# A four-layer network: two more turns in a fixed order, and nine shifted copies of the inverse norms

## The chip, the cores and the metric

The kernel runs on one core of a Trainium2 chip, as one launch over a batch of two images of 512 channels and 64 x 64 pixels. The metric is the device time of that launch in microseconds (us), the median of several runs.

## The reference

Four layers, each with a residual and a group normalisation ahead of it. The change lies in the first, an attention over a 3 x 3 neighbourhood and 256 pooled tokens. Cut to that part:

```python
x = x + L0(_gn(x))        # then L1, L2, L3 in the same way
# L0: B=2, C=512, N=64*64 pixels, 8 heads of 64, ws=3, ll=9
q = heads(xf @ W_q + b_q);  q_norm = q / norm(q)
q_scaled = (q_norm + query_embedding) * softplus(temperature)
k_l, v_l = split(xf @ W_kv + b_kv);  k_l = k_l / norm(k_l)     # per head and pixel
k_local, v_local = 3x3 patches of k_l, v_l (zero padded)
attn_local = einsum('bhnd,bhndk->bhnk', q_scaled, k_local)     # nine taps
attn_pool = einsum('bhnd,bhpd->bhnp', q_scaled, l2norm(k_pool))  # 256 pooled tokens
attn = softmax(concat([attn_local, attn_pool]))
lt = q_norm @ learned_tokens + learned_bias + attn[..., :ll]
out = (einsum(lt, v_local) + einsum(attn[..., ll:], v_pool)) @ W_proj + b_proj
```

All values are f32.

## The kernel before

**Units and turns.** `Local.run` (from L2047) does the first layer. The 512 channels are four chunks of 128 (two heads each), the 4096 pixels four strips of 1024 (`UT`), so an image has 16 units of one chunk and one strip, numbered by `u = 4 * chunk + strip`. A turn `i` runs from -4 to 16 and works on several units at once: it projects k and q for unit i+3 (`projections`), brings the inverse norms of what the turn before projected (`norms`, `normed`), forms the nine products of q with shifted k for unit i+1 (`tap_products`, DVE, L2489), sums each product over a head's channels on TensorE (`tap_sums`, L2527), projects v for unit i+1 (`value`), attends with unit i (`attend`: exponentials L2555 and L2559, values L2565, softmax sums L2581 and L2584, reciprocal L2609 to L2617) and weighs the neighbouring values of unit i-1 (`weigh`). Each of these is a generator; `in_turn` advances them in rotation, one step each.

**Orders.** Which instruction stands where on an engine is set by a scheduler, except in turns for which `self.steady` is true: there PE's instructions keep the order in which the generators emit them (`manual_schedule` for PE). `self.steady` also selects another plan of steps: products in pairs of taps (one DVE instruction of 128 x 2048 elements in place of two of 128 x 1024), `halved(1)` into the buffers `sq[2:]` in place of `prob`, other numbers of empty steps, and in `projections` the steps at which k, q and v are projected (`made`, `taken`). Before the change turns 1 to 11 are steady. Turn 13 projects no k and q, and v for the last two units. Turns 14 to 16 attend with the last units and multiply the outputs with the projection (`output`, L2258); `fetch_output` in turn 13 loads that projection into the four `sq` buffers.

**Buffers.** `mm` is a ring of five PSUM banks that nearly everything shares, `tap` is one bank for the tap sums, `qs` two for the q of the products. A tap sum ends with a DVE multiplication by the inverse norms (L2536) and an exponential on ACT (L2538), after which its bank is free. In `weigh`, each of the ten rows of weights of a unit is fetched by two broadcasting DMAs (L2640) into one of three buffers, copied to PSUM by ACT (L2656), multiplied on DVE (L2664) and added by POOL (L2669).

**Inverse norms.** The norm of k belongs to a pixel and a head, and each tap needs it at the neighbour's place. `inverse` is a tensor in device memory. `norms` makes the inverse square roots of a half strip (512 pixels) and stores them by one DMA into six rows: two heads by three shifts in x (L2434). `tap_inverses` reads, for each of four strips of partitions and each of three shifts in y, six rows (L2513): twelve DMAs a unit. Both ends of each row are set to zero at the beginning (L2134). All DMAs here are issued in order by SP.

Of the kernel before, what the change touches and what calls it, by code (L numbers as in the profile page):

```python
# [9 lines left out]
F32 = mybir.dt.float32  # L10
# [8 lines left out]
KC = C // P  # L19
W = 64  # L20
N = W * W
TB = 512
# [20 lines left out]
def bcast(ap, axis, n):  # L43

    a = ap.unsqueeze(axis)
    shape = list(a.shape)
    shape[axis] = n
    return a.to_broadcast(shape)


def in_turn(*gens):


    gens = list(gens)
    while gens:
        gens = [g for g in gens if next(g, gens) is not gens]
# [1911 lines left out]
class Local:  # L1968
# [9 lines left out]
    def __init__(self, net, X, Y, sp_scale, d, wp, yp, pp, ppt, pps):  # L1978
        self.net, self.nc, self.vec, self.cst = net, net.nc, net.vec, net.cst
        self.X, self.Y, self.sp_scale, self.d = X, Y, sp_scale, d  # L1980
        self.wp, self.pp, self.ppt, self.pps = wp, pp, ppt, pps
        nc, new = self.nc, lambda shape, name: wp.tile(shape, F32, name=name)

        self.yd = yp.tile([P, KC, N], F32, name="yd")
        self.edge = W + 1
        self.inverse = yp.tile([6 * KC, N + 2 * self.edge], F32, name="inverse")
        self.wd = yp.tile([3, P, KC, C], F32, name="wd")
        self.rows = cycle([yp.tile([P // 2, self.UT], F32, name=f"rows{i}") for i in range(2)]).__next__

        R = W + 2  # L1990
        flat = Y.rearrange("p k n -> p (k n)")
        self.next_w = flat[:, :KC * C].rearrange("p (kc o) -> p kc o", kc=KC)
        whole = Lent(flat)
        self.kx, self.vx = (whole.take([P, R, R]) for _ in range(2))
        qs, self.kraw = whole.take([P, 3 * self.UT]), whole.take([P, self.UT])
        self.qs = [qs[:, i * self.UT:(i + 1) * self.UT] for i in range(3)]
        weighed = whole.take([P, 2 * self.UT])

        self.taps = ([weighed[:, i * self.UT:(i + 1) * self.UT] for i in range(2)]
                     + [new([P, self.UT], "tap2")])  # L2000
        self.prods = [new([P, 2, self.UT], f"prods{i}") for i in range(2)]
        self.tok = whole.take([P, KC, 32])
        late = new([P, 13 * TB + 3 * TB], "late")
        part = Lent(late)
        self.prob = part.ring([P, TB], 4)
        self.att = part.ring([P, self.UT], 2)
        self.els = part.ring([P, TB], 2)

        self.halves = [part.take([P, TB]) for _ in range(2)]
        self.recip = part.take([P, TB])  # L2010
        self.lts = part.ring([P, TB], 3)

        self.first = Lent(late[:, :12 * TB])
        self.gelus = Lent(late[:, 13 * TB:]).ring([P, TB], 3)
        self.raw_w = [w.rearrange("p (kc o) -> p kc o", kc=KC)
                      for w in (weighed, flat[:, 6144:8192])]
        self.w_sr = qs[:, :KC * C].rearrange("p (kc o) -> p kc o", kc=KC)
        self.fold = flat[:, :6144].rearrange("p (i kc o) -> p i kc o", i=3, kc=KC)
        self.kp = new([P, KC, NK], "kp")
        self.vp = new([P, 2, C], "vp")  # L2020
        self.qn = whole.take([P, self.UT])
        self.w3 = new([P, 3, KC, P], "w3")
        self.sq = [new([P, TB], f"sq{i}") for i in range(4)]
        self.half = new([P, 32], "mhalf32")
        self.qb = new([P, KC], "qe_scaled")
        self.bias = {i: new([P, KC], "b_" + i) for i in "qkv"}
        self.w, self.lt, self.el, self.out = {}, {}, {}, {}
        load = lambda w, src: nc.sync.dma_start(w, src.rearrange("(kc p) o -> p kc o", p=P))
        load(self.w_sr, d["W_sr"])
        for i, src in enumerate((d["W_q"], d["W_kv"][:, :C], d["W_kv"][:, C:])):  # L2030
            load(self.fold[:, i], src)
        for i in range(2):
            load(self.raw_w[i], d["W_kv"][:, i * C:(i + 1) * C])
        nc.sync.dma_start(self.tok, d["tok32"])
        nc.vector.memset(self.half, -0.5)

        nc.vector.tensor_tensor(self.qb, self.vec[:, V_QE:V_QE + KC], sp_scale, ALU.mult)
# [9 lines left out]
    def run(self):  # L2047


        self.nmean = self.net.stats[:, 0]  # L2050
        xs = self.pooled_tokens()
        heads = self.pooled_heads(xs)
        units = KC * self.UN
        unit = lambda u: u if 0 <= u < units else None
        self.pending = []
        for i in "qkv":
            self.fetch(i, 0)
        for i in range(-4, units + 1):
            made, ahead, u, before = (unit(i + n) for n in (3, 1, 0, -1))
            self.steady = 1 <= i < units - 4  # L2060
            streams, ended = [], []
            stages = [self.norms(streams, ended)]
            if ahead is not None:
                stages.append(self.tap_products(ahead))
            if u is not None:
                stages.append(self.attend(u))
            if i == units:
                stages.append(self.output(KC - 2))
            if before is not None:
                stages.append(self.weigh(before))  # L2070
            if ahead is not None:
                stages.append(self.tap_sums(ahead))
            values = ([ahead] if i > 0 and ahead is not None else
                      {-4: [0], -2: [1]}.get(i, []))
            stages.append(self.projections(made, values, streams))
            stages.append(self.normed(ended))
            if i < -2:
                stages.append(islice(heads, 12 if i == -4 else None))
            if i == units - 3:
                stages.append(self.fetch_output())  # L2080
            if units - 3 < i < units:
                stages.append(self.output(i - units + 2))
            if self.steady or i == units:
                with self.net.tc.manual_schedule(engines={mybir.EngineType.PE}):
                    in_turn(*stages)
            else:
                in_turn(*stages)

        self.nc.sync.dma_start(self.next_w, self.d["w_q1"].rearrange("(kc p) o -> p kc o", p=P))
        in_turn(self.output(KC - 1))  # L2090
# [3 lines left out]
    def pooled_tokens(self):  # L2094

        net, nc, w = self.net, self.nc, self.w_sr
# [11 lines left out]
        for blk in range(NB):  # L2108
# [14 lines left out]
            if 1 <= blk <= 3:  # L2123
                i = blk - 1
                w3 = self.fold[:, i]
                net.scale_part(w3, slice(0, KC))
                at = (V_BQ, V_BK, V_BK + KC)[i]
# [2 lines left out]
                nc.sync.dma_start(self.wd[i], w3)  # L2130
        self.frame(self.kx)
        nc.gpsimd.memset(self.kraw[:, :TB], 0.0)
        for at in (0, self.edge - 1 + N):
            nc.sync.dma_start(self.inverse[:, at:at + self.edge + 1],  # L2134
                              self.cst[:6 * KC, :self.edge + 1])
        return xs

    def pooled_heads(self, xs):
# [220 lines left out]
    def projections(self, u, uvs, streams):  # L2359

        nc = self.nc
# [23 lines left out]

            uvs = [last - 1, last]
        values = [(u, j) for u in uvs for j in range(2)]
        made, taken = ((4, 6, 7, 8), (0, 2)) if self.steady else ((6, 7, 8, 9), (0, 3, 6, 9))
        for step in range(10):
            if step in made:  # L2390
                i = made.index(step)
                project("kq"[i // 2], i % 2)
            if step in taken and values:
                v, j = values.pop(0)
# [5 lines left out]
    def norms(self, streams, ended):  # L2400


        nc, wp = self.nc, self.wp
# [10 lines left out]
        n, a = (ps.rearrange("p (b r) -> p b r", r=32)[:, :, 2 * i:2 * i + 2] for i in range(2))  # L2414
# [11 lines left out]
        for s, (which, u, j, part, _) in enumerate(before):  # L2426
            row = rows[32 * s:32 * s + 2, :]
            if which == "q":
                ended.append((s, row, u, j, part))
                continue  # L2430
            at = self.edge + 1 + u % self.UN * self.UT + j * TB
            a = self.inverse[u // self.UN * 6:][:2, at:at + TB]
            heads, cols = a.ap
            nc.sync.dma_start(bass.AP(a.tensor, a.offset, [heads, [2 * heads[0] - 1, 3], cols]),  # L2434
                              bcast(row, 1, 3))
        yield

    def normed(self, ended):
# [67 lines left out]
    def tap_inverses(self, u):  # L2506

        inverse = (self.kraw[:, :TB] if u < KC * self.UN - 1
                   else self.w3[:, 2].rearrange("p k o -> p (k o)"))
        for q in range(4):  # L2510
            for dy in range(3):
                at = u % self.UN * self.UT + q // 2 * TB + dy * W + 1
                self.nc.sync.dma_start(inverse[32 * q + 6 * dy:][:6, :],  # L2513
                                       self.inverse[u // self.UN * 6:][:6, at:at + TB])
        return inverse

    def tap_sums(self, u):
# [348 lines left out]
```

## Time and profile before

| | |
|---|---|
| median of 3 runs | 5019.44 us (5018.50 to 5019.69) |
| profiled execution, its own time | 5015.88 us |
| its span | 5014.0 us, granted TensorE clock 0.984 |
| PE (matmul) busy | 4771.4 us, 95% of the span |
| VectorE (DVE) busy | 3074.1 us, 61% |
| ScalarE (ACT) busy | 1816.8 us, 36% |
| GpSimd (POOL) busy | 1859.1 us, 37% |
| inverse stores and reads | 64 and 384 DMAs of 12 KB |

Busy times are sums over one profiled execution. A row of the table by stretches, used below, gives the start and end of a stretch, its length, then for each engine the busy time and in brackets the number of records, the granted clock of TensorE (PEclk, 1.00 is full speed), the mean busy share of the 16 DMA engines, and GB/s. A 512-column f32 matmul leaves two records, and matmuls on different column strips overlap. A row of waits gives engine and instruction, what ended the wait, the sum in us, how often and the longest. A row of the timeline gives start, length, engine, line, operation, tiles, and in square brackets the idle time ahead of it and what ended it.

### The profile page before, as it was taken

How to read it: one execution, taken by the hardware profiler on the slowest of the kernel's cores; microseconds unless marked ns; L12 is line 12 of the kernel's file. 1: busy time of each engine (PE TensorE's matmuls, PEld its weight loads, DVE VectorE, ACT ScalarE, POOL GpSimd, SP SyncE). 2: the span in 40 equal slices, each digit the busy share in tenths (PEclk: the TensorE clock that was granted, in tenths of full speed). 3: DMA queues.
4: the chain of work that ended last, by engine and by line, in shares of the span. 5: the costliest groups of instructions: out<-in, count | busy, mean ns of one | idle time of the engine just before them, and what ended most of it. 6: DMA issues, size and time to landing. Idle time of an engine off the chain costs nothing. (4 is left out here: it accounts for less than half of the span.)

```text
span 5014.0 us, 48290 instructions
## 1 busy us (share of the span) xinstructions
PE 4771.4 (95%) x16883; PEld 1971.8 (39%) x16883; DVE 3074.1 (61%) x3958; ACT 1816.8 (36%) x3477; POOL 1859.1 (37%) x1220
## 2 busy tenths in 40 slices
PE   7999998999999999999999999989999999999998
PEld 3433332554334444433343333335543344444333
DVE  4367776744679533477732777767446794335776
ACT  1256664244323233322112566642443242333221
POOL 0046665501320145554500466654014101554554
PEclk9999999999999999999999999999999999999999
DMA  3035555500000000211120455555000000000111
GB/s 154 1 103 155 155 156 164 160 19 10 1 17 0 1 1 1 72 55 44 58 74 2 126 154 157 151 159 150 12 10 1 17 1 1 1 1 24 43 45 43
DMA packets 129440, 313.29 MB, mean 62 GB/s; under 512 B 23394, under 2 KB 36194, under 8 KB 127652
## 3 DMA queue, kind: packets, MB, share of 16 engines
q1 hardware_dynamic: 129188, 310.12, 21.6%
q8 instruction: 135, 2.21, 0.2%
q14 instruction: 117, 0.96, 0.1%
HBM read 260.73 MB, written 49.31 MB: 62 GB/s over the span
## 5 line engine op out<-in xcount | busy, mean ns | idle before, releaser
L134 PE MATMUL mm<-big,w 128*128 128x512 f32 x2496 | 1164.9, 610 | 16.3 <-DVE big L2448 11.5
L134 PEld LDWEIGHTS mm<-big,w 128*128 128x128 f32 x2496 | 452.6, 191 | 698.3 <-issue 557.2
L2669 POOL TENSOR_TENSOR late<-late,big 128x1024 f32<-128x1024 f32 x194 | 458.5, 2363 | 223.4 <-DVE big L2664 185.4
L2489 DVE TENSOR_TENSOR prods<-qs,big 128x1024 f32<-128x1024 f32 (+1 forms) x200 | 332.2, 1686 | 60.1 <-PE tap L2527 49.1
L1669 POOL TENSOR_TENSOR big<-big 128x512 f32<-128x512 f32 x224 | 277.8, 1273 | 219.4 <-ACT big L1660 219.4
L2664 DVE TENSOR_TENSOR big<-big,mm 128x512 f32<-128x512 f32 x388 | 253.1, 681 | 114.9 <-ACT mm L2656 107.0
L1660 ACT ACTIVATE big<-mm,ed 128x256 f32<-128x256 f32 x512 | 193.5, 489 | 233.1 <-DVE top L1656 200.7
L2656 ACT COPY mm<-big 128x512 f32<-128x512 f32 x432 | 245.8, 597 | 60.4 <-DMA big<-rows 25.1
L2574 POOL TENSOR_TENSOR late<-late 128x512 f32<-128x512 f32 x84 | 105.3, 1275 | 410.5 <-ACT late L2559 393.9
L2669 POOL TENSOR_TENSOR late<-late,tap 128x1024 f32<-128x1024 f32 x94 | 222.1, 2363 | 94.5 <-DVE tap L2664 80.1
L1472 POOL TENSOR_TENSOR wq<-prob 128x512 f32<-128x512 f32 x48 | 71.6, 1515 | 487.9 <-ACT prob L1469 476.5
L1656 DVE TENSOR_REDUCE top<-mm 128x1 f32<-128x512 f32 x256 | 159.0, 684 | 148.1 <-PE mm L1587 148.1
L1924 PE MATMUL mm<-k,w 128*128 128x512 f32 x512 | 235.1, 602 | 12.4 <-DVE k L1917 7.5
L134 PE MATMUL mm<-big,wq 128*128 128x512 f32 x512 | 236.7, 608 | 2.7 <-ACT off_t L1243 2.7
L1215 PE MATMUL mm<-big,wo 128*128 128x512 f32 x512 | 238.1, 611 | 0.0
L1382 PE MATMUL acc<-big,diag 128*128 128x512 f32 x512 | 228.7, 604 | 9.8 <-ACT diag L1387 4.6
L1634 PE MATMUL mm<-w,big 128*128 128x512 f32 x512 | 234.5, 601 | 0.0
L973 POOL TENSOR_TENSOR group_stats<-group_stats,cst 128x1 f32<-128x1 f32 (+1 forms) x20 | 20.2, 1025 | 566.4 <-DVE group_stats L972 510.2
L2527 PE MATMUL tap<-prods,cst 128*32 128x512 f32 x1152 | 189.6, 620 | 29.2 <-ACT late L2538 26.5
L1914 DVE RECIPROCAL psD<-psD 128x512 f32<-128x512 f32 x64 | 215.1, 3362 | 1.9
L134 PE MATMUL mm<-big,big 128*128 128x512 f32 x464 | 201.7, 594 | 0.5 <-DVE b_sr L1011 0.5
L1469 ACT ACTIVATE prob<-mm 128x512 f32<-128x512 f32 x256 | 133.2, 603 | 171.4 <-PE mm L1466 171.1
(428 smaller groups left out, 8114.1 us busy)
## 6 DMA issues: line engine op xcount, KB each, us to landing
big<-rows SPq DMA_DIRECT2D x432, 256.0 KB
tap<-rows SPq DMA_DIRECT2D x208, 256.0 KB
yd<-late SPq DMA_DIRECT2D x32, 512.0 KB
lost_all<-lost SPq DMA_DIRECT2D x128, 128.0 KB
out<-big SPq DMA_DIRECT2D x64, 256.0 KB
big<-in_W_kv SPq DMA_DIRECT2D x8, 1024.0 KB
rows<-late SPq DMA_DIRECT2D x64, 128.0 KB
big<-in_x SPq DMA_DIRECT2D x32, 256.0 KB
```

The costliest lines, as they stand in the source:

```text
L134: self.nc.tensor.matmul(ps, w[:, kc, :], X[:, kc, blk * TB:(blk + 1) * TB], start=(kc == 0), stop=(kc == KC - 1))
L1215: nc.tensor.matmul(ps, w[:, kc, oc * P:(oc + 1) * P], att[:, kc, :], start=(kc == 0), stop=(kc == KC - 1))
L1382: nc.tensor.matmul(accs[b], dg, src[:, b * TB:(b + 1) * TB], start=(j == 0), stop=(j == 6))
L1634: nc.tensor.matmul(ps, X[:, kc, lo:lo + P], wv[:, kc, :], start=(kc == 0), stop=(kc == KC - 1))
L1660: nc.scalar.activation(f[:, t, :], pS[h][i][:, t % 2, :], AF.Exp, bias=ed[:, t, 2 * cc + h:2 * cc + h + 1])
L1669: nc.gpsimd.tensor_tensor(a, a, part, ALU.add)
L1914: nc.vector.reciprocal(psD, psD)
L1924: nc.tensor.matmul(ps, self.wo[:, kc, oc * P:(oc + 1) * P], qs[:, kc, :], start=(kc == 0), stop=(kc == KC - 1))
L2489: self.nc.vector.tensor_tensor(self.pair(u, k)[:, :n].rearrange("p k (y x) -> p k y x", x=W), bcast(qs.rearrange("p (y x) -> p y x", x=W), ...
L2656: nc.scalar.copy(ps, part)
L2664: nc.vector.tensor_tensor(part.rearrange("p (y x) -> p y x", x=W), self.vx[:, y:y + self.UY // 2, dx:dx + W], ps.rearrange("p (y x) -> p y ...
L2669: nc.gpsimd.tensor_tensor(out, out, t, ALU.add)
```

## The change

`self.steady` holds two turns longer, for turns 1 to 13. In a steady turn up to four value projections find a place (steps 0, 2, 4, 6 instead of 0, 2), which turn 13 uses. `inverse` grows from 6 to 18 rows a chunk: a half strip is stored by three DMAs, one for each shift in y, so that all nine shifted copies stand in memory, and a read takes all 18 rows at once, four DMAs a unit in place of twelve. The zeroed ends grow to fit.

```diff
         self.edge = W + 1
-        self.inverse = yp.tile([6 * KC, N + 2 * self.edge], F32, name="inverse")
+        self.inverse = yp.tile([18 * KC, N + 2 * self.edge], F32, name="inverse")
...
             made, ahead, u, before = (unit(i + n) for n in (3, 1, 0, -1))
-            self.steady = 1 <= i < units - 4
+            self.steady = 1 <= i < units - 2
...
-        for at in (0, self.edge - 1 + N):
-            nc.sync.dma_start(self.inverse[:, at:at + self.edge + 1],
-                              self.cst[:6 * KC, :self.edge + 1])
+        for at in (0, N):
+            nc.sync.dma_start(self.inverse[:, at:at + 2 * self.edge],
+                              self.cst[:18 * KC, :2 * self.edge])
...
-        made, taken = ((4, 6, 7, 8), (0, 2)) if self.steady else ((6, 7, 8, 9), (0, 3, 6, 9))
+        made, taken = ((4, 6, 7, 8), (0, 2, 4, 6)) if self.steady else ((6, 7, 8, 9), (0, 3, 6, 9))
...
-            at = self.edge + 1 + u % self.UN * self.UT + j * TB
-            a = self.inverse[u // self.UN * 6:][:2, at:at + TB]
+            at = 2 * self.edge + u % self.UN * self.UT + j * TB
+            a = self.inverse[u // self.UN * 18:][:2, at:at + TB]
             heads, cols = a.ap
-            nc.sync.dma_start(bass.AP(a.tensor, a.offset, [heads, [2 * heads[0] - 1, 3], cols]),
-                              bcast(row, 1, 3))
+            row_at = heads[0]
+            for dy in range(3):
+                nc.sync.dma_start(bass.AP(a.tensor, a.offset + dy * (6 * row_at - W),
+                                          [heads, [2 * row_at - 1, 3], cols]), bcast(row, 1, 3))
...
         for q in range(4):
-            for dy in range(3):
-                at = u % self.UN * self.UT + q // 2 * TB + dy * W + 1
-                self.nc.sync.dma_start(inverse[32 * q + 6 * dy:][:6, :],
-                                       self.inverse[u // self.UN * 6:][:6, at:at + TB])
+            at = self.edge + u % self.UN * self.UT + q // 2 * TB
+            self.nc.sync.dma_start(inverse[32 * q:][:18, :],
+                                   self.inverse[u // self.UN * 18:][:18, at:at + TB])
```

Lines behind L2434 move by one to three in the changed kernel: L2513 becomes L2514, L2527 L2528, L2555 L2556 and so on; lines ahead of it stay.

## The prediction

> **What bounds the kernel now.** I read the page's busy times first (PE 95% of the span), so a gain has to come out of TensorE's time or its gaps. Then I cut the end of layer 0 at the last softmax-sum matmul (L2584) of each turn, which closes turns 10 to 14 of the first image at 701.75, 743.24, 789.14, 839.46 and 891.85 us, and asked for the busy time of every engine in these stretches:
>
> ```profile
> core 0: us, PE busy (x) PEld busy (x) DVE busy (x) ACT busy (x) POOL busy (x), PEclk, DMA share, GB/s
> 701.75:743.24 41.49, 40.79 (x151) 12.87 (x149) 32.50 (x48) 25.45 (x45) 26.26 (x14) 1.00 0.57 150
> 743.24:789.14 45.90, 45.09 (x162) 14.02 (x160) 34.82 (x55) 26.67 (x47) 28.57 (x15) 1.00 0.52 145
> 789.14:839.46 50.32, 46.00 (x151) 14.58 (x149) 32.25 (x53) 24.98 (x44) 26.05 (x14) 0.93 0.57 157
> 839.46:891.85 52.39, 42.83 (x138) 18.48 (x136) 34.59 (x47) 18.13 (x33) 31.64 (x17) 0.90 0.67 186
> ```
>
> The first row is a steady turn: 41.49 us long, PE busy for 40.79 of them, DVE for 32.5. The next two, turns 12 and 13 in the order that the scheduler chose, hold about the same matmuls (162 and 151 records against 151) and last 45.90 and 50.32 us. In the second image the same stretches last 41.47, 45.03 and 49.94 us.
>
> The same stretches for the nine-tap sums (L2527) alone show one part of the excess:
>
> ```profile
> 701.75:743.24 41.49, 5.31 (x36) 0.77 (x36) 1.00 0.57 150
> 743.24:789.14 45.90, 8.27 (x48) 1.29 (x48) 1.00 0.52 145
> 789.14:839.46 50.32, 8.06 (x36) 1.18 (x36) 0.93 0.57 157
> ```
>
> 36 records cost 5.31 us when they come in fours on four column strips, 8.06 us when the scheduler lets one or two in at a time. TensorE's waits from 743 to 892 us and the timeline ahead of the longest show the other part:
>
> ```profile
> PE tap L2527 <- ACT late L2538: 12.8, 3, 8.2
> PE mm L2258 <- ACT late L2559: 0.7, 1, 0.7
> ...
> 844.36 2.37 DVE L2616 TENSOR_TENSOR late<-late 128x512 f32<-128x512 f32 x1
> 846.77 0.69 DVE L2617 TENSOR_TENSOR late<-late 128x512 f32<-128x512 f32 x1
> 847.38 0.69 DVE L2536 TENSOR_TENSOR tap<-tap,big 128x512 f32<-128x512 f32 x1
> 848.10 0.60 ACT L2538 ACTIVATE late<-tap 128x512 f32<-128x512 f32 x1 [6.83 <-DVE tap L2536]
> 848.75 3.65 PE L2527 MATMUL tap<-prods,cst 128*32 128x512 f32 x16 [8.23 <-ACT late L2538]
> ```
>
> There is one tap bank. The next unit's tap sums wait for the exponential (L2538) of the last unit's, this for L2536, and L2536 stands on DVE behind the whole softmax-reciprocal chain (L2609 to L2617). In turn 13 PE so loses 4.23 us (at 798.07), after it 8.23 us.
>
> **What the Trainium skill says.** "TensorE: Matmul & The Clock Gate", section "What's actually happening": an idle window of about 3.4 us halves the PE clock. The trace agrees: PEclk is 1.00 in steady turns, 0.93 and 0.90 in the rows with the 4.23 and 8.23 us gaps. The same page, "Part 3: Packing small matmuls", section "The mechanism": matmuls on different column strips overlap. The trace agrees: 36 tap records in 5.31 us is 0.15 us each, while a record by itself lasts at least 0.59. "DMA: Bandwidth & Descriptors", section "Two DMAs through the same engine are not ordered": a dependent DMA is issued only when the first one's semaphore has come. The trace agrees: SP holds the second strip's store back until the first has landed (below).
>
> **The change, part by part.** *Turns 12 and 13 steady.* The built program's PE order in them is that of turn 11, matmul for matmul up to turn 13's sums: the four value projections at steps 0, 2, 4, 6 fill slots that steady turns already fill. So each should last a steady turn. First image: 45.90 + 50.32 - 2 x 41.49 = 13.2 us. Second: 45.03 + 49.94 - 2 x 41.47 = 12.0 us. Sum **25.2 us**. DVE's nine products become four pairs and a single at 2.28 us a pair against 2 x 1.22: nothing, and DVE has 9 us of slack in a steady turn.
>
> *The hand-over to turn 14*, which the scheduler still orders. At the end of turn 13's sums the old order has 12 tap records behind it that the new one has not (about 2 us of PE), and unit 15's first four products come before, not after, the reciprocal chain. But PE is starved there anyway, so DVE sets the pace. New DVE chain from the sums' end: 6.2 us to the first L2664 (as in the steady turn, 701.75 to 707.91), six more pairs' halves of L2664 0.6 each, nine single products 1.15 each, L2536 0.6, two L2661 1.2: 6.2 + 3.6 + 10.4 + 0.6 + 1.2 = 22.0 us. Old: 839.46 to the end of L2661 at 862.36 is 22.9 us. Nothing gained or lost, within 1 us; PE stays ill-fed for some 15 us, so a half clock remains there as now. PE idle of about 3.6 us is left before unit 15's first tap sum, then short waits for products.
>
> *SP in turn 13 to 14.* The projection weights for two of the four sq buffers now wait for the sums (which read sq as halves); first use (L2258) is some 25 us later: nothing. The store of unit 12's rows (L2675) moves ahead of the first tap fetches of unit 13. It waits for POOL's last sum, 15.4 us after the sums' end in a steady turn; with 0.4 issue, 4.7 landing and 1.2 copies the fetch is ready at 21.7, against L2661 at 20.8: up to 1 us an image.
>
> *Inverse norms.* 64 stores become 192 and 384 reads become 128, 128 SP issues fewer at about 0.29 us: 37 us of SP time, but SP's waits in a steady turn are for POOL (16.1 us of 41.5), so worth nothing. Three times the stored bytes is 0.8 to 2.4 MB of 313. The two edge fills are larger but come at 38 to 50 us, first read at 251: hidden. The stores also stand closer together:
>
> ```profile
> 729.12 0.43 SPq L2434 DMA_DIRECT2D inverse<-sq  x1
> 730.41 1.08 SPq L2640 DMA_DIRECT2D big<-rows  x2
> 732.10 0.24 SPq L2434 DMA_DIRECT2D inverse<-sq  x1
> 735.14 1.08 SPq L2640 DMA_DIRECT2D big<-rows  x2
> ```
>
> The second strip's store goes 2.98 us after the first, when that one has landed. Now a tap fetch goes in between; in the new order all six stores stand together, so that this fetch (730.41) leaves at about 733.3, some 2.9 us late, in every steady turn. It lands 4.6 us later, at 737.9, where its copy (L2656) runs at 736.98 today; the new ACT order puts these copies after the qs copies (L2483), which follow the last product and so end near 741.7. The PSUM bank that they take (a ring of five, counted through the turn) is freed by L2664 at 740.00 today, some 2.9 us later then, and the matmul that takes it next (L134 at 743.24) has 3.24 us of slack. I take 0 per turn, with -0.1 (fewer issues) and +0.3 as ends, over 22 old steady turns: -2 to +7 us.
>
> *Sum.* The profiled execution took 5015.88 us (span 5014.0): 5015.88 - 25.2 = 4990.7 us. The median of the runs, 5019.44, is 3.6 us above it, so **4994 us**.
>
> **The rivals.**
> 1. *Forecast: the gain of turns 12 and 13 stands at the end.* For it: turns 14 to 16 are PE work behind that front (44.4 of 48.4 us busy in turn 15), and the reciprocal chain, taps and stores all start from the same sums. 4988 to 4999 us. Chance 0.70.
> 2. *Part is given back after turn 13.* Late tap fetches, the half clock running into the first output matmuls (up to 5 us an image at half speed costs 2.5 us), or output loads that the earlier start uncovers. At 3 to 7 us an image: 5000 to 5009 us. Against it: the chain above comes out even. Chance 0.17.
> 3. *The six stores block SP.* The late tap fetch holds its PSUM bank past the 0.3 us that is left, PE waits in each steady turn. Price: from 1.15 us a turn over 22 turns the gain is gone; at 2 us a turn 44 - 25 = 19 us slower, 5038 us. For it: the bank ring is five deep, and psD's slot has 0.96 us of slack after a tap's L2664 in the same step. Against it: the delayed fetch is the next tap's, and ACT's order has moved its copies back already. Chance 0.07 (half of it within 0.2%).
> 4. *Turns 12 and 13 don't reach a steady turn's length*, because turn 13 drains and starves: no more than a third of the gain, about 5012 us. Against it: turn 13 makes no k and q projections, but these would stand after its sums; what stands before them is turn 12's and complete. Chance 0.06.
>
> **How the numbers follow.** 0.2% of the time is 10 us, about what a measurement can tell: faster means under 5009, slower over 5029. Rivals 1 and 2 give faster 0.87; same 0.09 (rival 4 and half of 3); slower 0.04. Range: down to 4986 for a smoother hand-over (the 1 us above, and the half clock after the 8.23 us gap gone, some 2.5 us an image) and the lighter SP queue, up to 5007 over most of rival 2; about two in ten lie outside.
>
> **What would show it.** Right: the two stretches ending with turn 12's and 13's sums at 41.5 us each with PEclk 1.00 and 36 tap records in about 5.3 us; PE's wait for L2538 at 4.23 us gone, the 8.23 us one short, with waits for DVE's products (L2489) in its place; steady turns still 41.5 us; layer 1's first matmul (L134 on wq, now 1027.25 us) some 13 us earlier. Wrong: steady turns of 42 us or more with SP waiting on inverse stores (rival 3), turn 13 over 44 us (rival 4), or layer 1 starting less than 8 us earlier though turn 13's sums end 13 us earlier (rival 2).

## The result, and the profile after

The changed kernel takes 5031.57 us in the median of ten runs (5021.51 to 5039.03); the kernel before took 5018.35 us in ten runs beside it (5012.85 to 5020.48). The ratio is 1.0025, 95% interval 1.0017 to 1.0034: slower, by some 13 us, where 25 us of gain were forecast. The profiled execution took 5025.03 us (span 5023.2), so it is a quick one of its kind.

The same cut as before, at the last softmax-sum matmul of each turn (L2585 now), in the table by stretches, for turns 11 to 14 of the first image:

```profile
core 0: us, PE busy (x) PEld busy (x) DVE busy (x) ACT busy (x) POOL busy (x), PEclk, DMA share, GB/s
714.50:757.09 42.59, 40.86 (x148) 12.87 (x148) 32.89 (x48) 25.49 (x46) 26.25 (x13) 1.00 0.56 147
757.09:799.67 42.58, 40.85 (x148) 12.87 (x148) 32.90 (x48) 25.50 (x46) 26.28 (x13) 1.00 0.54 148
799.67:844.09 44.42, 41.97 (x149) 13.15 (x148) 32.88 (x48) 25.08 (x45) 27.49 (x14) 1.00 0.65 171
844.09:900.43 56.34, 48.72 (x150) 19.04 (x149) 41.10 (x54) 22.19 (x41) 33.92 (x17) 0.97 0.67 186
```

Turn 12 is a steady turn now and turn 13 nearly one. But a steady turn lasts 42.59 us in place of 41.49, with nearly the same PE busy time (40.86 against 40.79 us): the 1.1 us is a wait. And turn 14 lasts 56.34 us in place of 52.39.

The nine-tap sums did what was expected of them. Those of L2528 alone, in the first three of these stretches:

```profile
714.50:757.09 42.59, 5.31 (x36) 0.77 (x36) 1.00 0.56 147
757.09:799.67 42.58, 5.31 (x36) 0.78 (x36) 1.00 0.54 148
799.67:844.09 44.42, 5.31 (x36) 0.77 (x36) 1.00 0.65 171
```

TensorE's waits in two steady turns of the changed kernel (671.91 to 757.09 us); in the kernel before such a stretch has only the like of the first and the last row:

```profile
PE mm L134 <- DVE big L2450: 1.0, 2, 0.5
PE mm L134 <- DVE big L2665: 1.0, 1, 1.0
PE mm L134 <- DVE tap L2665: 1.0, 1, 1.0
PE mm L134 <- ACT late L2560: 0.3, 2, 0.2
```

So once a turn the first projection matmul after the sums (L134) waits 1.0 us for a tap product (L2665). The timeline of the changed kernel ahead of that wait (only the rows that matter; tap 5 is the row of weights with `i` = 5 in `weigh`):

```profile
747.00 0.23 SPq L2436 DMA_DIRECT2D inverse<-sq  x1
747.33 2.68 SPq L2641 DMA_DIRECT2D big<-rows  x4
...
753.14 1.06 PE L2528 MATMUL tap<-prods,cst 128*32 128x512 f32 x8
754.25 1.23 DVE L2491 TENSOR_TENSOR prods<-qs,big 128x1024 f32<-128x1024 f32 x1 [1.06 <-PE tap L2528]
755.56 1.21 ACT L2485 COPY qs<-big 128x512 f32<-128x512 f32 x2 [1.68 <-DVE prods L2491]
756.01 1.08 PE L2585 MATMUL mm<-late,cst 64*64 64x512 f32 x4
756.70 2.14 ACT L2657 COPY mm<-big 128x512 f32<-128x512 f32 x4
757.38 1.88 DVE L2665 TENSOR_TENSOR big<-big,mm 128x512 f32<-128x512 f32 x3 [1.91 <-ACT mm L2657]
758.12 0.70 PE L134 MATMUL mm<-big,w 128*128 128x512 f32 x1 [1.03 <-DVE big L2665]
```

Read it from the bottom. L134 needs the PSUM bank that tap 5 holds; L2665 frees it at 758.06. L2665 waits for its copy (L2657, 756.70). The fetch for that copy was issued at 747.33 and both its halves had landed at 752.12; ScalarE was idle for 1.68 us until 755.56 and then ran the copies of qs first, because they come first in its order, and they wait for the ninth product (L2491), which waits for TensorE's tap sums. That ScalarE takes its instructions strictly in order is what the Trainium skill states ("PSUM — Partial Sum Buffer", section "Engine vs sequencer instructions"); the trace agrees: landed data waits 4.6 us (752.12 to 756.70) behind a copy that isn't ready.

In the kernel before, the end of the same turn (743.31 us) has both copies of tap 5 ahead of the ninth product and of the copies of qs, and L134 starts without a wait:

```profile
736.98 0.59 ACT L2656 COPY mm<-big 128x512 f32<-128x512 f32 x1
...
738.84 0.59 ACT L2656 COPY mm<-big 128x512 f32<-128x512 f32 x1
739.32 1.28 DVE L2664 TENSOR_TENSOR big<-big,mm 128x512 f32<-128x512 f32 x2
...
740.52 1.22 DVE L2489 TENSOR_TENSOR prods<-qs,big 128x1024 f32<-128x1024 f32 x1
...
741.77 1.21 ACT L2483 COPY qs<-big 128x512 f32<-128x512 f32 x2 [0.62 <-DVE prods L2489]
...
743.24 0.70 PE L134 MATMUL mm<-big,w 128*128 128x512 f32 x1
```

The account, after less before, from the turns' ends in both images: turns 12 and 13 give 9.2 and 8.7, together 18.0 us; turns 2 to 11 cost 12.1 + 11.2 = 23.3; turn 14 costs 3.9 + 3.7 and turn 15 2.3 + 0.8, together 10.8. Net +16.1 us; parts outside these turns are 6.9 us shorter, which leaves the 9.2 us between the two profiled executions. No run explains these 6.9 us; the ten runs of the kernel before alone lie up to 7.6 us apart.

### The profile page after: what moved, and what is told of

It reads as the page before. It is cut to its first block, busy times and chain, and to the rows that moved or that the text cites. A ratio compares the mean times of both kernels' runs of the same rounds, so it can differ in the third digit from the quotient of the medians.

```text
span 5023.2 us, 48217 instructions
## 1 busy us (share of the span) xinstructions
PE 4762.5 (95%) x16883; PEld 1966.3 (39%) x16883; DVE 3094.2 (62%) x3942; ACT 1820.4 (36%) x3477; POOL 1862.6 (37%) x1220
## 5 line engine op out<-in xcount | busy, mean ns | idle before, releaser
L134 PE MATMUL mm<-big,w 128*128 128x512 f32 x2496 | 1163.3, 609 | 47.1 <-DVE big L2665 16.5
L134 PEld LDWEIGHTS mm<-big,w 128*128 128x128 f32 x2496 | 451.3, 191 | 726.6 <-issue 553.8
L2670 POOL TENSOR_TENSOR late<-late,big 128x1024 f32<-128x1024 f32 x194 | 459.6, 2369 | 237.1 <-DVE big L2665 196.1
L2491 DVE TENSOR_TENSOR prods<-qs,big 128x2048 f32<-128x2048 f32 (+1 forms) x184 | 330.4, 1819 | 47.4 <-PE tap L2528 37.1
L2665 DVE TENSOR_TENSOR big<-big,mm 128x512 f32<-128x512 f32 x388 | 253.2, 681 | 117.0 <-ACT mm L2657 111.6
L2657 ACT COPY mm<-big 128x512 f32<-128x512 f32 x432 | 243.5, 592 | 119.9 <-DMA big<-rows 74.0
L2670 POOL TENSOR_TENSOR late<-late,tap 128x1024 f32<-128x1024 f32 x94 | 221.9, 2361 | 116.3 <-DVE tap L2665 95.6
L134 PE MATMUL mm<-big,wq 128*128 128x512 f32 x512 | 236.7, 608 | 2.7 <-ACT off_t L1243 2.7
L1382 PE MATMUL acc<-big,diag 128*128 128x512 f32 x512 | 228.7, 604 | 10.1 <-ACT diag L1387 4.6
L134 PE MATMUL mm<-big,big 128*128 128x512 f32 x464 | 201.7, 594 | 0.5 <-DVE b_sr L1011 0.5
L2528 PE MATMUL tap<-prods,cst 128*32 128x512 f32 x1152 | 187.8, 610 | 12.4 <-ACT late L2539 9.8
```

Source lines behind the costliest of these rows:

```text
L134: self.nc.tensor.matmul(ps, w[:, kc, :], X[:, kc, blk * TB:(blk + 1) * TB], start=(kc == 0), stop=(kc == KC - 1))
L1382: nc.tensor.matmul(accs[b], dg, src[:, b * TB:(b + 1) * TB], start=(j == 0), stop=(j == 6))
L2491: self.nc.vector.tensor_tensor(self.pair(u, k)[:, :n].rearrange("p k (y x) -> p k y x", x=W), bcast(qs.rearrange("p (y x) -> p y x", x=W), ...
L2657: nc.scalar.copy(ps, part)
L2665: nc.vector.tensor_tensor(part.rearrange("p (y x) -> p y x", x=W), self.vx[:, y:y + self.UY // 2, dx:dx + W], ps.rearrange("p (y x) -> p y ...
L2670: nc.gpsimd.tensor_tensor(out, out, t, ALU.add)
```

## The experiments

Theory A: the steady extension is a gain, and the inverse norms' three-way stores cost 1.1 us in every steady turn, by the order that the scheduler builds around them. Rival B: the extension is what costs. Within A, A1 says that the place of tap 5's copies in ScalarE's order decides, A2 that the late fetch behind six stores does. The two kernels and all seven experiments in one table (turns and start of layer 1 of the first image, from their traces; the ratio is to runs of the kernel before on the same chip, whose medians are 5018.35, 5016.9 and 5016.4 us):

| kernel | median us | ratio, 95% interval | turns 2 to 11 | 12, 13 | 14 | layer 1 starts |
|---|---|---|---|---|---|---|
| before | 5018.35 | 1 | 41.5 | 45.9, 50.3 | 52.4 | 1027.2 |
| changed | 5031.57 | 1.0025 (1.0017 to 1.0034) | 42.6 to 43.3 | 42.6, 44.4 | 56.3 | 1036.5 |
| steady_only | 4994.15 | 0.9956 (0.9943 to 0.9970) | 41.5 | 41.5, 41.5 | 57.3 | 1019.1 |
| inverse_only | 5033.25 | 1.0033 (1.0021 to 1.0045) | 42.6 to 43.1 | 46.5, 50.2 | 49.4 | 1036.5 |
| stores_apart | 5006.52 | 0.9980 (0.9973 to 0.9987) | 41.6, three 42.5 to 42.7 | 41.6, 44.6 | 51.9 | 1025.7 |
| copies_first | 4998.56 | 0.9965 (0.9953 to 0.9977) | 41.5 | 41.5, 41.5 | 56.7 | 1016.7 |
| store_behind | 4986.36 | 0.9945 (0.9932 to 0.9959) | 41.5 | 41.5, 41.5 | 51.6 | 1012.2 |
| copies_store | 4996.24 | 0.9964 (0.9952 to 0.9976) | 41.5 | 41.5, 41.8 | 54.2 | 1017.6 |
| reads_split | 5034.42 | 1.0035 (1.0021 to 1.0048) | 42.6 to 42.9 | 42.6, 43.2 | 57.8 | 1035.5 |

### steady_only: one half of the change

```diff
 (to the kernel before)
-            self.steady = 1 <= i < units - 4
+            self.steady = 1 <= i < units - 2
-        made, taken = ((4, 6, 7, 8), (0, 2)) if self.steady else ((6, 7, 8, 9), (0, 3, 6, 9))
+        made, taken = ((4, 6, 7, 8), (0, 2, 4, 6)) if self.steady else ((6, 7, 8, 9), (0, 3, 6, 9))
```

> The kernel before with its steady turns extended through turn 13, and the inverse norms as they were (six rows, one store per strip, twelve reads). Theory A (the three-way stores lengthen every steady turn by 1.1 us, by way of the late copies of tap i=5; the steady extension itself is a gain): turns 1 to 12 last 41.5 us, turn 13 42.5 to 43.5, turn 14 some 54 to 56 and turn 15 48 to 50, since the hand-over gives a part back; layer 1 starts 6 to 10 us earlier per image; 4998 to 5007 us. Rival B (the extension is what costs: its order or its hand-over): steady turns of 42.5 us here too, or layer 1 no earlier than before; 5018 us or more.

Measured: 4994.15 us, ratio 0.9956. Turns 12 and 13 last 41.5 us each; against before that is 13.3 us in the first image and 12.0 in the second, the 25.2 us of the prediction. Turn 14 takes 4.9 us more (57.27), 4.4 in the second image. Turn 13 was expected at 42.5 to 43.5 us and turn 14 at 54 to 56, so the first came out better and the second worse. Theory A stands for the extension, and the total lies 3.9 us below its range; rival B falls for the steady turns, and keeps the hand-over.

### inverse_only: the other half

```diff
 (to the changed kernel)
-            self.steady = 1 <= i < units - 2
+            self.steady = 1 <= i < units - 4
```

> The changed kernel with the steady turns ending at 11 again, so that the inverse norms alone are changed. Theory A: steady turns of 42.6 us with TensorE waiting 1.0 us in each for the bank of tap i=5 (L134 on L2665), turns 12 and 13 as before (46 and 50 us); over some 22 steady turns 5018 + 22 to 26, that is 5038 to 5046 us. Rival B: steady turns of 41.5 us, 5014 to 5020 us.

Measured: 5033.25 us, ratio 1.0033, some 16 us slower. Two of its steady turns (668.97 to 754.14 us) in TensorE's waits:

```profile
PE mm L134 <- DVE big L2450: 1.1, 2, 0.5
PE mm L134 <- DVE big L2665: 1.0, 1, 1.0
PE mm L134 <- DVE tap L2665: 1.0, 1, 1.0
PE mm L134 <- ACT late L2560: 0.3, 2, 0.2
```

The wait for L2665 is there once in each turn, without the steady extension, and the turns are 42.6 us. The total is 5 us under the expectation: turn 14 is 3.0 and 3.5 us shorter than before in the two images, against turn 13 of the second one, 3.9 us longer; the expectation left both out.

### stores_apart: a fetch between the two strips' stores

```diff
 (to the changed kernel)
         for s, (which, u, j, part, _) in enumerate(before):
+            if j:
+                yield
```

> The changed kernel with the second strip's three stores one step later, so that SP issues a tap fetch between the two strips' stores, as the kernel before does; in the order that the scheduler then builds, the copies of tap i=5 still stand behind the copies of qs on ScalarE in most turns. Theory A1 (the place of the copies in ScalarE's order decides): TensorE still waits in most steady turns, 42.0 to 42.6 us each, 5020 to 5032 us. Rival A2 (the late landing decides, the fetch standing behind six stores): turns back to 41.5 us, 5000 to 5008 us.

Measured: 5006.52 us, ratio 0.9980. Most steady turns are 41.56 us, and the wait for L2665 is gone. But the run doesn't tell A1 from A2, since its premise was wrong: in the order that was built the copies of tap 5 stand ahead of the copies of qs again (in turn 11 its first one runs at 742.42 and qs at 747.21); those of tap 6 stand behind. What it does show is that this order isn't built when a fetch stands between the stores; that it is their standing together which makes it is inferred from this run alone, in which one generator also takes one step more. The turns of 42.5 us wait up to 1.3 us in another place, for ScalarE's exponentials (L134 on L2562); in one such turn these run at 476.46, right behind a tap copy that waited 1.25 us for its fetch.

### copies_first: the order of the copies alone

```diff
 (to the changed kernel)
+        copied = getattr(self, "copied", None)
+        held = self.net.tc.issue_after(copied) if self.steady and copied else nullcontext()
+        with held:
             (the two copies of qs)
...
-                nc.scalar.copy(ps, part)
+                copy = nc.scalar.copy(ps, part)
+                if i == 5:
+                    self.copied = copy.ins
```

> The changed kernel with one order forced: the copies of qs (L2485) stand behind the copies of tap i=5 (L2657) on ScalarE, as in the kernel before; the six stores still stand together on SP. Theory A1 (the copies' place decides): the copies run when the fetch lands, about 752.2 where turn 11's sums end at 757.1, so L2665 ends some 2 us before those sums and L134's wait is gone: steady turns of 41.5 to 41.7 us, 5000 to 5008 us. Rival A2 (the late landing decides): the wait stays, 42.3 us or more a turn, 5025 us or more.

Measured: 4998.56 us, ratio 0.9965; steady turns of 41.48 us. The timeline of the same place in this kernel (its turn 11 ends at 742.68; L2660 is the tap copy, L2670 the tap product, L2488 the copy of qs; again only the rows that matter):

```profile
728.48 4.00 SPq L2436 DMA_DIRECT2D inverse<-sq  x6
732.59 3.01 SPq L2644 DMA_DIRECT2D big<-rows  x4
739.36 1.11 ACT L2660 COPY mm<-big 128x512 f32<-128x512 f32 x2
739.84 1.23 DVE L2494 TENSOR_TENSOR prods<-qs,big 128x1024 f32<-128x1024 f32 x1 [1.06 <-PE tap L2531]
740.98 1.27 DVE L2670 TENSOR_TENSOR big<-big,mm 128x512 f32<-128x512 f32 x2
741.10 1.21 ACT L2488 COPY qs<-big 128x512 f32<-128x512 f32 x2 [0.62 <-DVE prods L2494]
741.60 1.08 PE L2588 MATMUL mm<-late,cst 64*64 64x512 f32 x4
742.61 1.55 PE L134 MATMUL mm<-big,w 128*128 128x512 f32 x3
```

All six stores still stand together and the fetch still leaves behind them, 10.1 us ahead of the turn's end (732.59 to 742.68; 9.8 in the changed kernel, 12.9 in the kernel before). Yet the copies run at 739.36, ahead of the ninth product, L2670 ends at 741.65, and L134 starts at 742.61 with no wait of its own. Same late transfer, no cost: A1 is shown, and A2 falls. The median lies 1.4 us below the expected range.

### reads_split: stores or reads

```diff
 (to the changed kernel)
-            self.nc.sync.dma_start(inverse[32 * q:][:18, :],
-                                   self.inverse[u // self.UN * 18:][:18, at:at + TB])
+            for dy in range(3):
+                self.nc.sync.dma_start(inverse[32 * q + 6 * dy:][:6, :],
+                                       self.inverse[u // self.UN * 18 + 6 * dy:][:6, at:at + TB])
```

> The changed kernel with its six stores per turn, but with twelve reads of six rows per unit, as before, in place of four of eighteen. If the stores make the order that costs 1.1 us a turn: steady turns of 42.5 us again, TensorE waiting at L134 for L2665, 5025 to 5036 us. If the reads do (fewer on SP, so other work moves up): turns of 41.5 us, 4996 to 5006 us.

Measured: 5034.42 us, ratio 1.0035, steady turns of 42.6 us. TensorE's waits from 300 to 700 us:

```profile
PE mm L134 <- DVE big L2666: 6.2, 6, 1.0
PE mm L134 <- DVE big L2450: 4.7, 9, 0.5
PE mm L134 <- DVE tap L2666: 3.4, 3, 1.3
```

Nine waits, 9.6 us in all, the same as in the changed kernel in this window. The four reads in place of twelve have no part in the loss of the steady turns.

### store_behind: the hand-over to turn 14

In steady_only, turn 14's longest wait is 4.5 us at L2565. It is for L2661, the product with a unit's first row of weights. The timeline ahead of it:

```profile
844.85 2.36 POOL L2669 TENSOR_TENSOR late<-late,big 128x1024 f32<-128x1024 f32 x1
847.24 0.33 SPq L2675 DMA_DIRECT2D yd<-late  x1
847.74 1.12 SPq L2640 DMA_DIRECT2D big<-rows  x2
...
852.70 1.11 ACT L2656 COPY mm<-big 128x512 f32<-128x512 f32 x2 [8.28 <-DMA big<-rows]
853.32 1.29 DVE L2661 TENSOR_TENSOR late<-late,mm 128x512 f32<-128x512 f32 x2 [5.32 <-ACT mm L2656]
...
854.66 1.12 PE L2565 MATMUL mm<-late,vp 128*64 128x512 f32 x2 [4.50 <-DVE late L2661]
```

SP holds the store of unit 12's rows (L2675) at the head of its queue until POOL's last sum ends at 847.21; the tap fetch behind it leaves at 847.74 and lands 4.9 us later (852.60), and ScalarE, DVE and TensorE wait in a row. In this experiment the store goes behind the two fetches, as in every earlier steady turn:

```diff
 (to steady_only)
-        self.fetch_tap(u, 1)
+        self.fetched = self.fetch_tap(u, 1)
         yield
...
-        nc.sync.dma_start(self.yd[:, cc, lo:lo + self.UT], out)
+        with self.net.tc.issue_after(self.fetched) if self.steady else nullcontext():
+            nc.sync.dma_start(self.yd[:, cc, lo:lo + self.UT], out)
```

> The steady extension alone, with the inverse norms of before, as in the run steady_only, and one order on SP forced in it: the store of a unit's rows (L2675) goes behind the next unit's first two tap fetches in turn 13 too, as it does in every earlier steady turn. Theory C (this store, which waits 9.8 us for POOL at the head of SP's queue, holds back the tap fetches on which L2661 and so L2565 wait; TensorE stands 4.5 us there, DVE 5.3 us): turn 14 falls from 57.3 to 52 to 53.5 us and layer 1 starts 3.5 to 5 us earlier in each image; 4983 to 4989 us. Rival D (DVE's work sets turn 14, the wait only moves): turn 14 stays within 1 us, 4992 to 4997 us.

Measured: 4986.36 us, ratio 0.9945, the fastest kernel here: its slowest run (4990.16) is below the fastest of steady_only (4991.86), though these ran on another chip. The same place in its timeline (L2677 is the store, L2662 what was L2661):

```profile
838.81 1.11 SPq L2640 DMA_DIRECT2D big<-rows  x2
...
843.88 1.11 ACT L2657 COPY mm<-big 128x512 f32<-128x512 f32 x2 [1.99 <-DMA big<-rows]
844.70 0.33 SPq L2677 DMA_DIRECT2D yd<-late  x1
845.38 1.27 DVE L2662 TENSOR_TENSOR late<-late,mm 128x512 f32<-128x512 f32 x2
```

The fetch leaves at 838.81, 13.4 us after the sums' end (825.42), not 19.8. Turn 14 in the table by stretches, first in steady_only, then here:

```profile
827.95:885.22 57.27, 47.24 (x149) 18.95 (x149) 37.76 (x49) 19.82 (x37) 34.33 (x17) 0.94 0.64 183
```

```profile
825.42:876.98 51.56, 45.69 (x149) 18.69 (x149) 37.48 (x49) 19.32 (x35) 34.35 (x17) 1.00 0.70 204
```

Same work, 5.71 us less: TensorE is idle for 4.16 us less (the 4.5 us wait is gone, other gaps are a little longer) and busy for 1.55 us less, since with no wait over 1.8 us left the granted clock is 1.00 instead of 0.94. That agrees with what the Trainium skill says of idle windows ("TensorE: Matmul & The Clock Gate", section "What's actually happening"). But turn 15 of the same kernel shows that no single long wait is needed:

```profile
891.07:894.48 3.41, 1.88 (x6) 0.60 (x7) 2.75 (x5) 3.22 (x7) 0.70 (x1) 1.00 0.85 262
894.48:897.89 3.41, 3.41 (x9) 1.04 (x6) 1.29 (x2) 1.18 (x3) 3.41 (x3) 0.50 0.89 264
```

The clock is halved here after 3.41 us in which TensorE was busy for 1.88 us and waited no longer than 1.53 us at once. Theory C is shown, with turn 14 even below its range of 52 to 53.5 us; D falls. Layer 1 starts 7.0 us earlier than in steady_only, more than was expected, but 2.5 us of that lie ahead of turn 1 and aren't the store's.

### copies_store: both orders forced in the changed kernel

Its edit is that of copies_first and that of store_behind together.

> The changed kernel with both orders forced: the copies of qs behind those of tap i=5 on ScalarE, and the store of a unit's rows behind the next unit's first two tap fetches on SP. If the two causes are separate and these are all there is, it is the run copies_first less what the store costs: steady turns of 41.5 us, turn 14 of 52 to 53.5 us, 4987 to 4993 us, and no slower than store_behind by more than 6 us. If the nine-copy inverse norms cost something beyond the order of the copies, it stays 8 us or more above store_behind; if they bring something, it is below it.

Measured: 4996.24 us, ratio 0.9964: no gain over copies_first that the intervals can tell, and some 10 us over store_behind. Turn 14 is 2.5 us shorter than in copies_first, but turn 15 is longer (51.9 against 47.7 us in the first image, 51.3 against 49.7 in the second). In this order the tap sums of turn 14 wait 4.9 us for the exponential of the one tap bank (L2531 on L2542), as they do in the changed kernel, where store_behind's longest such wait is 1.8. So the nine-copy inverse norms still cost something when the steady turns are free of them, at the hand-over. TensorE's longest waits from 820 to 890 us:

```profile
PE tap L2531 <- ACT late L2542: 4.9, 1, 4.9
PE mm L134 <- DVE tap L2671: 1.0, 1, 1.0
```

The trace shows where this begins. The two forced orders hold for what a steady turn emits, and the copies of qs at the end of turn 13 belong to turn 14 already. So they run ahead of the tap copies once more (824.74 against 825.88 us), two pairs of tap products stand ahead of the reciprocal chain, and that chain starts 2.7 us after the sums' end instead of 0.05 (store_behind); the multiplication (L2540) that the exponential waits for ends 11.7 us after it instead of 7.4. In turn 15 the store (L2683, 892.25) stands ahead of the first tap fetch (892.74), which leaves 12.3 us after the sums' end instead of 6.9, and TensorE waits 4.8 us for the product with the first row (L2668) instead of 1.5. That these two orders make up the 10 us was not tried.

## Why the prediction was wrong

- **Turns 12 and 13 become steady: right.** 25.2 us were worked out, and 25.2 us is what steady_only shows in these turns. In the changed kernel 18.0 us of it arrive: both turns pay the 1.1 us, and turn 13 another 1.1 to 1.8.
- **Inverse norms, "I take 0 per turn": the step that failed.** Measured 1.1 us a steady turn, 23.3 us over turns 2 to 11 of both images (turn 1 is not lengthened). The chain that could cost was named rightly: copies that come late, the bank that they take, and L134 with 3.24 us of slack. Its length was read off wrongly. The prediction has the copies of qs "end near 741.7". In the timeline of before that is where they begin: the ninth product ends at 741.74, and they run from 741.77 to 742.98. From 741.7, tap 5's copy (0.6 us) and L2664 (0.7 us) would end at 743.0. That fits the prediction's other reading, "some 2.9 us later" than 740.00, and stays just within the slack. From 742.98 they end at about 744.3, which is 1.06 us behind L134's start at 743.24; the trace shows 1.03. So what sets L2664's time is the end of the copies of qs, not the lateness of the fetch, and it was put 1.3 us too early. The upper end of +0.3 us a turn left no room for that, so that the range missed as well.
- **Rival 3 had the price and the bank, not the cause.** It said that from 1.15 us a turn the gain would be gone. SP's blocking is real (the fetch is late), but copies_first keeps it at no cost in the steady turns. The argument against it, "ACT's order has moved its copies back already", was the very thing that cost.
- **The hand-over, "nothing gained or lost, within 1 us": wrong by 4.9 and 4.4 us** (steady_only). The prediction saw that the store moves ahead of the tap fetches, and put 15.4 us for POOL's last sum "in a steady turn" into a turn that isn't one: DVE runs products and L2536 ahead of the first L2664 there, which comes 9.6 us after the sums, not 6.2. POOL's sum ends at 19.3 us and L2661 starts at 25.4, not 20.8. "Up to 1 us an image" measured 5.3 us of DVE's idle time, and store_behind takes it back.
- **SP's fewer issues worth nothing: right, as far as the runs can tell** (reads_split, 5027 to 5036 us, against 5022 to 5039 for the changed kernel). **Tap sums of 5.31 us, PEclk 1.00 in turns 12 and 13: right.** The 8.23 us wait became 4.92, where some 3.6 were forecast.
- The forecast of 4994 us is what steady_only takes, to a microsecond, but that is luck in part: this kernel loses some 9 us in turn 14, which were not forecast, and its profiled execution makes up some 6 us of them in parts that neither kernel changes (from the start of layer 1 in the second image to the end it takes 1492.3 us against 1498.5; the other seven take 1494.5 to 1495.4).

## What to carry to other kernels

Where a scheduler writes each engine's order, an edit to a few transfers can cost through the order of engines that it doesn't touch: compare the built orders and, for every instruction that changed places, work its new time from the end of what now stands ahead of it, not from its old time plus the delay of its data. Where two delays could use up a slack, work out both and compare the later one with it. At the edge of a hand-ordered stretch, look at what stands at the head of the DMA queue: a store that waits for the end of a chain must not stand ahead of the fetch that the next chain starts with.

## What was not expected of the hardware

In the changed kernel the first strip's three small stores (from 742.90 us) land 3.2 to 3.4 us after their issue, the second strip's (from 746.36) 1.5 to 1.8 us. A tap fetch was issued at 742.27, 0.6 us ahead of the first three, and landed at 746.15, just before the second three were issued. In stores_apart, where the second three go out 1.7 us after a tap fetch that is still in flight (issued 736.36, landed 740.12), they take 2.8 to 2.95 us. So in these cases a small store took up to twice as long when a fetch ahead of it on the queue had not landed; no run here took the cause apart.
